# Two instruction orders and one split load in a two-layer adapter, attention and router kernel

## The chip, the cores and the metric

The kernel runs on one core of a Trainium2 chip. The metric is the device time of one execution in microseconds (us); for a kernel timed several times it is the median. A profiled execution of the same program gives the trace that all times of single instructions come from; its span, from the first to the last instruction, is a little shorter than its device time.

## The reference

The input x has 8 batches of 128 tokens with 512 features, float32. What is computed, cut to what matters:

```python
# layer 0
c = einsum('bsi,boi->bso', x, weight[adapter_ids])            # one 512 x 512 matrix per batch
x = x + c @ base_w.T + base_b + 2 * (top-2 gated sum of 8 rank-16 experts on c)
# layer 1, attention: 32 query heads, 8 key/value heads, head size 128
q, k, v = x @ Wq.T, x @ Wk.T, x @ Wv.T
q, k = rope(rmsnorm(q)), rope(rmsnorm(k))                      # positions start at cache_seqlens
kc, vc = k_cache[block_table], v_cache[block_table]            # 16 pages of 32 tokens per batch
o = softmax(mask(q @ concat(kc, k).T / sqrt(128))) @ concat(vc, v)
o = o @ Wo.T
# layer 1, router: 64 experts of rank 8, top 16
x = x + 2 * ((o @ A_w.T) * gate(o)) @ B_w.T
```

## The kernel before

**Stages.** The first stage (L0, lines 367 to 648) goes over the 8 batches: product with the batch's adapter matrix (`l0_adapter`, L494), copy (L503), products with the gate and low-rank matrix (L511) and the base matrix `bww` (L516), expert gating, and the new x, normed by a power of two and transposed into `xo` (L578). The second stage (L1, lines 751 to 1073) is the attention, the third (lines 1076 to 1145) the end of the router. The whole instruction order is written out by hand: each engine executes its instructions in the order in which the code emits them, and waits on semaphores where data or buffers need it.

**Loads of L0.** `l0_load(b)` issues on SyncE (SP) the transposed x of a batch (`xT`, L377; for batch 0 on ScalarE's queue) and its adapter matrix (L382), chosen by a register. Batch 0's matrix is loaded in two halves of its columns, all others whole. Behind batch 0's matrix SP issues `glw`, `bww`, then batch 1's `xT` and matrix.

**Units and turns.** Attention is cut into 32 steps (4 pairs of key/value heads by 8 batches) and each step into 2 units, 64 units in all; unit u belongs to step `u // 2`. Call `iteration(u)` turn u. Turn u does, for its unit's 4 query heads: `scores` (L788 against the cached keys `kt`, L791 against the new keys), `mask_exp` (L801 on VectorE reads the scores, adds the mask and takes the row minimum; L812 on ScalarE is the exponential), `normalize` (L817 on VectorE, L818 on GpSimd) and `blocks` (L823, a transpose of 32 x 32 blocks on VectorE into the tile `pb`). The scores of a head take a PSUM tile `s` of two; head 2 needs the tile of head 0, head 0 of the next unit that of head 2. When all four heads' blocks and a unit's rotated q and k (`blocks_qk`, L774) are in `pb`, `exchange_out` (L835) writes it to DRAM in four DMAs, two issued by SP and two by ScalarE; this tile in DRAM is `px`. In the next turn `exchange_in` (L845, L848) reads it back as `qkb` (q and k of the unit two after) and `pT`. There is one `pb`, so `blocks_qk` of a turn waits until the last turn's `px` has landed.

**What else a turn holds.** `values` (L868) of the unit two before, `evict_o` (L879, ScalarE, tile `oT`) and `output` (L890) of the unit three before, `project` (L259: q, k and v of units to come, three or four of seven products of a scheme that multiplies sums of halves) and `heads_qk` (L855, ScalarE: `qkb` to `qkT`, which the next turn's scores read). At the end of turn u stand `norms(u + 3)` and `rotate(u + 3)`:
- `norms`: five squares with a sum (L308) and a scaled copy `vn` (L310) on ScalarE, then on GpSimd mean and epsilon (L312, `ss`) and the power -0.5 (L314, `rs`);
- `rotate`: on VectorE L326 twice for q, L340 twice for k (these need `rs`), L343 and L344. It reads tables that `make_tables` (L233) makes on GpSimd. Its result is read by `blocks_qk(u + 3)` in turn u + 1.

The order at the end of a turn is: `normalize` of head 3, `norms`, `blocks` of heads 2 and 3, `exchange_out`, `rotate`. In turns 0 to 2 `project_whole` (L292) stands in place of `project`. `sums_q` (L163, VectorE) adds quarters of a projection matrix; `sums_x` (L168 to L171, GpSimd) does so for x.

**Keys and values.** The 16 key pages of the next step are gathered one DMA each by SP (`gather`, L193 and L194), 8 in each of a step's two turns: three at the turn's start, then `exchange_in`'s two DMAs, which wait for `px`, then five. Value rows come by GpSimd (`gather_v`, L204). `load_y` (L143) and the store of y (L914) are issued by SP in a step's first turn, after the pages and before `exchange_out`. Projection matrices of the next pair of heads are loaded by GpSimd (`load_q`, L153) in four turns of every sixteen.

The lines that decide the order of the pages:

```python
first = u % GH * NPP // GH                 # GH = 2, NPP = 16
if pages:
    gather(st + 1, first, first + 3)
if on(u - 1):
    exchange_in(u - 1)
if pages:
    gather(st + 1, first + 3, first + NPP // GH)
```

Of the kernel before, what the change touches and what calls it, by code (L numbers as in the profile page):

```python
# [16 lines left out]
P = 128  # L17
B = 8
S = 128
DM = 512  # L20
# [6 lines left out]
PAGES, PSIZE, NPP = 64, 32, 16  # L27
# [3 lines left out]
GH = 2  # L31
# [26 lines left out]
def adaln_ffn_kernel(  # L58
# [59 lines left out]
        out=nw, in_=norm_w.rearrange("o (t d) -> o t d", t=2).to_broadcast([P, 2, D])  # L118
# [39 lines left out]
    def sums_q(g, *tees):  # L158

        w = wq_t[g]  # L160
        for t in tees:
            to, x, y = {3: (5, 3, 1), 2: (4, 5, 0), 4: (6, 2, 4), 1: (1, 1, 0)}[t]
            nc.vector.tensor_tensor(w[:, to], w[:, x], w[:, y], ALU.add if t == 2 else ALU.subtract)  # L163
# [19 lines left out]
    def gather(step, first=0, end=NPP):  # L183
        hf, b = divmod(step, B)
        if first == 0:
            kv_t[step] = (
                kvp.tile([P, NPP, GH, PSIZE], F32, tag="kt", name=f"kt_{step}"),
                kvp.tile([P, LC, GH * D], F32, tag="vt", name=f"vt_{step}", bufs=3),
            )
        kt, vt = kv_t[step]  # L190
        for j in range(first, end):
            at = b * NPP + j
            page = nc.sync.value_load(pg[0:1, at : at + 1])  # L193
            nc.sync.dma_start(  # L194
                out=kt[:, j, :, :].rearrange("p g t -> p (g t)"),
                in_=kc[hf, ds(page, 1)].rearrange("o p f -> p (o f)"),
            )
# [26 lines left out]
    NU = len(units)  # L224
# [122 lines left out]
    def rotate(u):  # L347
        rotate_q(u)
        rotate_k(u)
# [17 lines left out]
    with ExitStack() as l0:  # L367
# [6 lines left out]
        def l0_load(b):  # L374
            xT = p2.tile([P, NC, S], F32, tag="xT", name=f"xT_{b}", bufs=3)
            eng = nc.scalar if b == 0 else nc.sync
            eng.dma_start(out=xT, in_=xt[b].rearrange("(c p) n -> p c n", p=P))  # L377
            wt = wt_home.pop(b)
            a = nc.sync.value_load(ids[0:1, b : b + 1])
            half = DM // 2 if b == 0 else DM  # L380
            for n in range(0, DM, half):
                nc.sync.dma_start(  # L382
                    out=wt[:, :, n : n + half],
                    in_=w0[ds(a, 1), :, n : n + half].rearrange("o (c p) n -> p (o c) n", p=P),
                )
            loaded[b] = [xT, wt]

# [49 lines left out]
        for i in range(QD):  # L437
            nc.gpsimd.dma_start(
                out=vpg[i * 32 : (i + 1) * 32], in_=vpages[i : i + 1].to_broadcast([32, B * LC])
# [311 lines left out]
    with ExitStack() as l1:  # L751
# [63 lines left out]
        def normalize(u, h):  # L815
            den = den_t.pop((u, h))
            nc.vector.reciprocal(den, den)  # L817
            nc.gpsimd.tensor_scalar(p_t[u, h], p_t[u, h], den, 1.0, ALU.mult, ALU.mult)  # L818
# [135 lines left out]
        def iteration(u):  # L954
# [16 lines left out]
                slots = (1, 2, 6) if four else (4, 5, 3)  # L971
            st = u // GH
            pages = on(u) and 1 < st + 1 < NQ * B
            first = u % GH * NPP // GH
            if pages:
                gather(st + 1, first, first + 3)
            if on(u - 1):
                exchange_in(u - 1)
            if pages:
                gather(st + 1, first + 3, first + NPP // GH)  # L980
            if pages:
                gather_v(st + 1, u % GH * LC // GH, (u % GH + 1) * LC // GH)
            if on(u + 3) and u % GH == 1:
# [12 lines left out]
            for h in range(REP):  # L996
                if on(u):
                    scores(u, h)
                    mask_exp(u, h)
                    if h > 0:  # L1000
                        normalize(u, h - 1)

                    if h == 1:
                        if u == 2:
                            sums_q(0, 1)
                        elif u == 3:
                            sums_q(1, 3, 2)
                        elif u == 4:
                            sums_q(1, 4, 1)
                        elif r in (10, 11, 12, 13) and u < NU - 8:  # L1010
                            sums_q(group + r // 12, *((3, 2), (4, 1))[r % 2])
                    if h == 2:
                        new_pb(u)
                        if u + 2 in range(3, NU):
                            blocks_qk(u + 2, u)
                    if h > 1:
                        blocks(u, h - 2)
                    if h == 1 and u == NU - 5:
                        f_fold(f[1])
                    if h == 2 and fb is not None:  # L1020
                        yT_t[fb] = f_turn(fb, *f)
                if on(u - 3):
                    output(u - 3, h)
                if h > 0 and slots:
                    project(k, j, slots[h - 1 : h])

                if u < 3 and h in (1, 3):
                    project_whole(1, *[(0, 1, h // 2), (1, h // 2, 1), (1, h // 2, 0)][u])
# [13 lines left out]
                load_o(group - 1, r * 2 - 2, r * 2)  # L1042
            if NU - 8 < u < NU - 2:
                f_weights(u - NU + 7)
            if on(u):
                normalize(u, REP - 1)
            if 3 < u + 3 < NU:
                norms(u + 3)
            if on(u):
                blocks(u, REP - 2)  # L1050
                blocks(u, REP - 1)
                exchange_out(u)
            if 3 < u + 3 < NU:
                rotate(u + 3)
                if four and slots:
                    project(k, j, (7,))
# [167 lines left out]
```

## Time and profile before

| | |
|---|---|
| Median of 3 runs | 1245.48 us (1244.46 to 1246.58) |
| Profiled execution | 1245.63 us |
| Its span | 1243.9 us |
| TensorE (PE) busy | 1225.1 us, 98% |
| VectorE (DVE) busy | 902.7 us, 73% |
| GpSimd (POOL) busy | 588.8 us, 47% |
| ScalarE (ACT) busy | 506.2 us, 41% |
| DMA moved | 298.99 MB, mean 240 GB/s |
| Granted TensorE clock, mean | 0.997 |

PE's weight loads (PEld) overlap its matmuls. A float32 matmul of the program shows as two records, so "x8" is four of them. In a timeline a line gives the start in us, the time in us, engine, source line and operation, output <- inputs, and in brackets how long the engine was idle before it and what released it. SPq and ACTq are DMA issues by SP and ScalarE. In a table of windows a line gives the stretch, its length, the busy time of PE, PEld, DVE, ACT and POOL, the granted PE clock, the DMA engines' busy share and GB/s. The releaser of a wait is inferred, and where several things were waited for it is the one that came last by the record.

### The profile page before, as it was taken

What the parts mean: (1) busy time and instruction counts of PE and PEld (TensorE: products, weight loads), DVE (VectorE), ACT (ScalarE), POOL (GpSimd) and SP (SyncE); (2) the same over time, 40 slices, a digit from 0 to 9 for tenths busy, and PEclk for the clock granted to TensorE, in tenths of its full rate; (3) what the DMA queues carried; (4) which work ended last, traced back from release to release, by engine and by line L of the source; (5) the groups of instructions that cost most, each with busy time, mean ns of one, the idle gap of its engine ahead of it and who ended that gap; (6) DMA issues with size and microseconds to landing.
All of it is one profiled execution on the core that took longest, in us unless ns stands there. A gap on an engine that the chain in (4) does not pass through costs nothing.

```text
span 1243.9 us, 15966 instructions
## 1 busy us (share of the span) xinstructions
PE 1225.1 (98%) x3851; PEld 650.3 (52%) x3851; DVE 902.7 (73%) x2045; ACT 506.2 (41%) x1457; POOL 588.8 (47%) x687
## 2 busy tenths in 40 slices
PE   9999899999999999999999999999999999999998
PEld 7765455544555555554555545555455555555444
DVE  2546798888877777788877777799777777787522
ACT  1334444444444444444444444444444444443211
POOL 2443465575544445554545544555545444553100
PEclk9999899999999999999999999999999999999999
DMA  9922777788777877888878877888878777887512
GB/s 302 303 79 94 224 235 247 246 272 284 254 239 255 262 250 240 282 287 259 279 246 263 254 251 246 290 280 278 259 244 287 244 235 230 258 280 256 185 51 85
DMA packets 211553, 298.99 MB, mean 240 GB/s; under 512 B 84547, under 2 KB 122180, under 8 KB 211460
## 3 DMA queue, kind: packets, MB, share of 16 engines
q1 hardware_dynamic: 179620, 205.69, 52.9%
q10 hardware_dynamic: 18960, 52.21, 11.9%
q0 software_dynamic: 12880, 40.08, 9.8%
q8 instruction: 31, 0.51, 0.2%
q14 instruction: 62, 0.51, 0.1%
HBM read 183.54 MB, written 114.36 MB: 239 GB/s over the span
## 4 chain that ended last, share of the span: by engine, by line
PE 89%; DMA 3%; DVE 3%; ACT 1%; issue 1%; POOL 1%; SPq 1%; ACTq 0%; DVEq 0%; POOLq 0%
PE o L868 20%; PE p L259 18%; PE s L788 17%; PE y L890 16%; PE s L791 4%; PE cp L494 2%; PE p L292 2%; PE bp L516 2%; PE op L1121 2%; DMA px<-pb 2%; PE fz L700 2%; DMA kt<-in_kc 1%; PE cp L511 1%; ACT sq L308 1%; DVE pb L823 1%
## 5 line engine op out<-in xcount | busy, mean ns | idle before, releaser
L818 POOL TENSOR_SCALAR p<-p,den 128x640 f32<-128x640 f32 x256 | 210.2, 821 | 427.1 <-DVE den L817 426.6
L812 ACT ACTIVATE p<-p,low 128x640 f32<-128x640 f32 x256 | 211.9, 828 | 442.8 <-DVE den L817 293.6
L801 DVE CUSTOM_DVE_ANT_0 p<-s,mask,rs 128x640 f32<-128x640 f32 x256 | 223.8, 879 | 114.5 <-PE s L791 111.4
L259 PE MATMUL p<-wqkv,xo 128*128 128x384 f32 x784 | 280.4, 486 | 0.0
L788 PE MATMUL s<-kt,qkT 128*128 128x512 f32 x504 | 257.9, 593 | 5.0 <-issue 2.5
L890 PE MATMUL y<-wo,oT 128*128 128x512 f32 x512 | 261.3, 595 | 1.2 <-ACT oT L879 1.2
L868 PE MATMUL o<-pT,vt 128*128 128x512 f32 x512 | 230.2, 592 | 0.0
L823 DVE STREAM_TRANSPOSE pb<-p 128x640 f32<-128x640 f32 x256 | 211.0, 824 | 17.0 <-POOL p L818 17.0
L259 PEld LDWEIGHTS p<-wqkv,xo 128*128 128x128 f32 x784 | 148.9, 190 | 139.8 <-issue 72.7
L791 PEld LDWEIGHTS s<-qkT 128*128 128x128 f32 x504 | 95.8, 190 | 120.6 <-issue 120.6
L868 PEld LDWEIGHTS o<-pT,vt 128*128 128x128 f32 x512 | 97.3, 190 | 110.3 <-issue 95.2
L204 POOL DMA_INDIRECT vt<-in_vc,vrow x128 | 136.1, 1063 | 39.7 <-issue 27.6
L788 PEld LDWEIGHTS s<-kt,qkT 128*128 128x128 f32 x504 | 94.8, 190 | 100.6 <-issue 57.5
L314 POOL TENSOR_TENSOR rs<-ss,mhalf 128x5 f32<-128x5 f32 x64 | 99.8, 1559 | 5.3
L308 ACT ACTIVATE sq<-c 128x128 f32<-128x128 f32 x320 | 98.8, 309 | 8.1
L791 PE MATMUL s<-qkT 128*128 128x128 f32 x504 | 96.8, 274 | 0.0
L879 ACT COPY oT<-o 128x512 f32<-128x512 f32 x64 | 37.5, 585 | 142.1 <-PE o L868 139.4
L890 PEld LDWEIGHTS y<-wo,oT 128*128 128x128 f32 x512 | 78.4, 192 | 6.5 <-issue 4.3
L262 DVE TENSOR_TENSOR c<-c,p 128x384 f32<-128x384 f32 x84 | 45.3, 539 | 30.4 <-PE p L259 30.4
L868 PE MATMUL o<-pT,vn 128*128 128x512 f32 x128 | 65.4, 592 | 0.0
L308 ACT ACTIVATION_READ_ACCUMULATOR sq<-c 128x1 f32 x320 | 59.7, 187 | 0.0
L340 DVE SCALAR_TENSOR_TENSOR ca<-c,rs,tab 128x128 f32<-128x128 f32 x64 | 24.4, 380 | 43.0 <-POOL rs L314 43.0
(180 smaller groups left out, 1205.7 us busy)
## 6 DMA issues: line engine op xcount, KB each, us to landing
pT<-px SPq DMA_DIRECT2D x64, 1280.0 KB, 6.6
px<-pb SPq DMA_DIRECT2D x122, 400.0 KB, 5.8
px<-pb ACTq DMA_DIRECT2D x122, 400.0 KB, 6.3
qkb<-px SPq DMA_DIRECT2D x61, 320.0 KB, 3.5
kt<-in_kc SPq DMA_DIRECT2D x512, 32.0 KB, 4.5
wqkv<-in_wqkv POOLq DMA_DIRECT2D x32, 384.0 KB, 5.6
yd<-ya SPq DMA_DIRECT2D x24, 256.0 KB, 2.0
wo<-in_wo POOLq DMA_DIRECT2D x12, 512.0 KB, 4.6
```

Source lines behind the costliest of these rows:

```text
L204: nc.gpsimd.indirect_dma_start(out=kv_t[step][1][:, c, :], out_offset=None, in_=vc, in_offset=bass.IndirectOffsetOnAxis(ap=vrow[:, hf, at ...
L259: nc.tensor.matmul(out=ps, lhsT=xo[:, pr, x, c, :], rhs=w[:, c, :], start=(c == 0), stop=(c == 1))
L308: nc.scalar.activation(sq, cs[:, at : at + D], AF.Square, accum_out=ss[:, h : h + 1])
L314: nc.gpsimd.tensor_tensor(rs, ss, mhalf, ALU.pow)
L788: nc.tensor.matmul(out=s[:, :L], lhsT=qkT[:, h, :], rhs=kt[:, :, g % GH, :], start=True, stop=True)
L791: nc.tensor.matmul(out=s[:, L:NK], lhsT=qkT[:, h, :], rhs=qkT[:, REP, :], start=True, stop=True)
L801: nc.vector.tensor_tensor_reduce(out=p, in0=s_t.pop((u, h))[:, :NK], in1=mask_t[st], scale=rs_t[u][:, h : h + 1], scalar=BIG, op0=ALU.add, ...
L812: nc.scalar.activation(p, p, AF.Exp, bias=low, scale=-1.0, accum_out=den)
L818: nc.gpsimd.tensor_scalar(p_t[u, h], p_t[u, h], den, 1.0, ALU.mult, ALU.mult)
L823: nc.vector.transpose(pb_t[u][:, :, h * w : (h + 1) * w].rearrange("p i (j a) -> p j i a", a=32), p_t.pop((u, h)).rearrange("p (j i a) -> ...
L868: nc.tensor.matmul(out=o, lhsT=vt[:, c, j * D : (j + 1) * D] if c < LC else vn_t.pop(u), rhs=pT[:, c], start=(c == 0), stop=(c == LC),)
L890: nc.tensor.matmul(out=y_t[st], lhsT=oT_t[u][:, h, :], rhs=wo_t[g][:, h, :], start=(h == 0 and j == 0), stop=(h == REP - 1 and j == GH - 1),)
```

## The change

Three things are changed; nothing is computed differently.

- Unit 4: `norms(4)` moves from the end of turn 1 to the end of turn 0, `rotate(4)` from the end of turn 1 into turn 2, behind `mask_exp` and `normalize` at head 1. The `sums_q(0, 1)` that stood there moves to the end of turn 2, before `normalize` of head 3.
- Key pages: 10 in a step's first turn (three, the exchange's two reads, seven) and 6 in its second (three and three), in place of 8 and 8.
- Batch 0's adapter matrix is loaded in four pieces of 128 columns in place of two of 256.

The matmuls of PE and their order stay the same.

```diff
-            half = DM // 2 if b == 0 else DM
-            for n in range(0, DM, half):
+            part = DM // 4 if b == 0 else DM
+            for n in range(0, DM, part):
                 nc.sync.dma_start(
-                    out=wt[:, :, n : n + half],
-                    in_=w0[ds(a, 1), :, n : n + half].rearrange("o (c p) n -> p (o c) n", p=P),
+                    out=wt[:, :, n : n + part],
+                    in_=w0[ds(a, 1), :, n : n + part].rearrange("o (c p) n -> p (o c) n", p=P),
                 )
...
-            first = u % GH * NPP // GH
+            first, end = ((0, 10), (10, NPP))[u % GH]
             if pages:
                 gather(st + 1, first, first + 3)
             if on(u - 1):
                 exchange_in(u - 1)
             if pages:
-                gather(st + 1, first + 3, first + NPP // GH)
+                gather(st + 1, first + 3, end)
...
                     if h == 1:
                         if u == 2:
-                            sums_q(0, 1)
+                            rotate(4)
...
+            if u == 2:
+                sums_q(0, 1)
             if on(u):
                 normalize(u, REP - 1)
-            if 3 < u + 3 < NU:
+            if u == 0:
+                norms(4)
+            elif 4 < u + 3 < NU:
                 norms(u + 3)
             if on(u):
                 blocks(u, REP - 2)
                 blocks(u, REP - 1)
                 exchange_out(u)
-            if 3 < u + 3 < NU:
+            if 4 < u + 3 < NU:
                 rotate(u + 3)
```

## The prediction

> **What bounds the kernel now.** I read the page first (busy shares, chain), then the waits of TensorE, then the timelines around each wait. One profiled execution ran 1245.63 us, its span is 1243.9; the three timed runs have the median 1245.48, 0.15 below it. I sum against 1245.63 and take 0.15 off at the end. Differences under 0.2% (2.5 us) can't be told from no change here.
>
> ```profile
> PE 1225.1 (98%) x3851; PEld 650.3 (52%) x3851; DVE 902.7 (73%) x2045; ACT 506.2 (41%) x1457; POOL 588.8 (47%) x687
> PE 89%; DMA 3%; DVE 3%; ACT 1%; issue 1%; POOL 1%; SPq 1%; ACTq 0%; DVEq 0%; POOLq 0%
> ```
>
> PE is busy 98%, and the change leaves its instructions and their order alone. So only PE's idle 18.8 us, and stretches at half clock, can be won. PE's waits (engine, line, releaser; total, times, longest) name what this change can touch:
>
> ```profile
> PE s L788 <- DVE low L801: 4.1, 1, 4.1
> PE s L788 <- issue: 2.5, 1, 2.5
> PE s L788 <- DMA px<-pb: 1.6, 1, 1.6
> PE cp L494 <- DMA wqkv<-in_w: 1.1, 1, 1.1
> PE s L788 <- DMA kt<-in_kc: 0.4, 1, 0.4
> ```
>
> The rest is start, tail and small L0 waits that no edit reaches.
>
> **Part A: unit 4's norms and rotation.** The 4.1 us are in turn 2. Scores of head 2 need the PSUM pair of head 0, freed by the masked read (L801) on DVE; that stands behind rotate(4) (L326 to L344), which waits for POOL's rs, which waits for ACT's five squares:
>
> ```profile
> 140.59 0.35 DVE L340 SCALAR_TENSOR_TENSOR ca<-c,rs,tab 128x128 f32<-128x128 f32 x1 [1.35 <-POOL rs L314]
> 142.04 0.88 DVE L801 CUSTOM_DVE_ANT_0 p<-s,mask,rs 128x640 f32<-128x640 f32 x1
> 142.99 2.07 PE L788 MATMUL s<-kt,wt 128*128 128x512 f32 x2 [4.09 <-DVE low L801]
> 146.00:147.00 1.00, 1.00 (x3) 0.34 (x2) 1.00 (x4) 0.49 (x1) 0.41 (x1) 0.50 0.32 17
> 148.00:149.00 1.00, 1.00 (x5) 0.60 (x4) 0.90 (x4) 0.00 (x0) 0.00 (x0) 1.00 1.07 369
> ```
>
> The last two are windows: third number from the end is PE's granted clock. After the stall PE ran at 0.50 until 147.8: 142.99 to 150.17 took 7.18 us, where the same two scores and one projection at full clock take 1.08 + 1.08 + 2.58 = 4.74. So the stall costs 4.09 + 2.44 = 6.5 us.
>
> After the change DVE leaves turn 1 at 138.0 and goes straight to L801 (0.80 from one to the next): 138.0 to 138.9, just as PE finishes its projection at 138.9. The stall is gone here. What the moved steps cost:
> - Turn 0: five squares (0.43 each) and vn (0.39) are 2.55 us of ACT, from 124.8 (end of a copy) to 127.3. Behind them on ACT are px(0)'s two DMA issues, now at 126.46. At 153.17 ACT issued such a DMA 0.25 before its vn began, so I expect 126.6: 0.15 late, at most 0.9 if it waits for vn. POOL's ss and rs (0.3 + 1.2) and the tables (1.45) then end at 129.9, so p(1,0) starts 1.2 after its present 128.63; its transpose runs only at 133.08, so that is covered.
> - Turn 2: rotate(4) is 2.7 us of DVE (137.98 to 139.23 and 140.59 to 142.04) between the reads of heads 1 and 2; it ends near 142.9, head 2's read 143.8. Then DVE needs pb free, which px(1) holds until it has landed.
> - sums_q(0,1) (1.3 mean) goes to turn 2's end; its reader comes in turn 4. Covered; it delays rotate(5) by about 1, but that waits for rs(5).
>
> What is late next is the exchange:
>
> ```profile
> 145.45 0.54 SPq L845 DMA_DIRECT2D qkb<-px  x1
> 150.75 0.73 ACT L855 COPY qkT<-qkb 128x640 f32<-128x640 f32 x1
> 154.66 0.59 ACT L879 COPY oT<-o 128x512 f32<-128x512 f32 x1 [0.86 <-PE o L868]
> 158.68 0.87 DVE L801 CUSTOM_DVE_ANT_0 p<-s,mask,rs 128x640 f32<-128x640 f32 x1
> ```
>
> px(1) leaves when turn 1's blocks are done (138.0) and lands at 145.4. Nothing in the change hastens that. Then qkb(3) (median 3.5 + 0.5 queue), ACT's copy to qkT(3) from 149.4 to 150.1. PE, freed of the stall, would be ready for turn 3's scores at 148.2: it waits 1.9. Then ACT does norms(5) (2.45 us), two issues (0.8), and only then oT(0): ready at 153.6, where PE could use it at 151.2: another 2.4. rs(5), rotate(5) and L801 of unit 3 follow qkT(3): 150.1 instead of 151.45, so that read ends at 158.2 where it now ends at 159.55. PE started its third score pair at 159.63, right behind it. So of 6.5 us only 1.3 is left. The two new waits lie 1 us apart in a stretch of 5.4 us, and the clock may fall again: PE stopped at 138.9 and by the windows 0.50 was granted from about 140.9, 2.0 us later. Then PE's 4.1 us of work from 153.6 to that score pair takes up to 2.4 more, as after 142.99, or half of that; it would end at 157.7, so 0.55 is cover. That leaves a gain of 0.7 or a loss of 0.5. Bounds for A: gain 1.3 to loss 2.2 (all 4.1 us at half clock, third pair at 161.8). I take a gain of 0.6, near the middle case.
>
> [...]
>
> **Part B: ten pages, then six.** The waits at 307.11 (1.57), 575.00 (2.46) and 874.70 (0.38) are first scores of a step, behind turns in which weights are loaded. PE there needs qkT, which ACT had ready 4 us before, and kt. The releaser names ("issue", px) are not what feeds it; the last pages are:
>
> ```profile
> 565.52 3.71 SPq L194 DMA_DIRECT2D kt<-in_kc  x5
> 575.00 1.10 PE L788 MATMUL s<-kt,qkT 128*128 128x512 f32 x2 [2.46 <-issue]
> ```
>
> Five issues in 3.71 us are 0.84 apart, so the last left at 568.9, 6.1 before PE started. With two pages fewer behind qkb and pT, the last leaves 1.69 sooner. If it lands 1.69 sooner: 307.11 wins all 1.57, 575.00 wins 1.69 of 2.46, 874.70 all 0.38: 3.6 us. Bounds: nothing (landing set by pT's 1.28 MB and the weights ahead of it, not by issue) to 4.4 (lighter queue, all gone). I take 3.6: in the chain the last page before 874.70, issued at 870.15, landed 4.30 later, the median landing of all pages (4.5), so issue time decided there.
> Cost: in even turns SP issues 7 pages after pT, 1.69 more, ahead of load_y, the y store and px. Where pages end at 281.8 and px leaves at 287.61 that is covered. The tightest are turn 2 (pages to 150.9, px 152.00: 0.6 late) and the turn with pages to 854.1, y store 855.01, px 855.88: 0.8 late. That px carries q and k two turns ahead: px of 152.00 was read back at 159.98 and copied by ACT only at 167.84. So nothing; without that cover, 1.4 in all.
>
> **Part C: the first adapter matrix in four.** PE starts cp(0) at 8.04 after 1.06 idle. A 256 KB piece needs fewer bytes before it lands, so the first product could start up to 1.06 earlier. But:
>
> ```profile
> 13.67 0.30 PEld L516 LDWEIGHTS bp<-bww,cT 128*128 128x128 f32 x2 [0.16 <-DMA bww<-in_base_w]
> 17.24 0.37 SPq L377 DMA_DIRECT2D xT<-in_xt  x1
> 17.38 1.95 PE cp L494 x16
> ```
>
> PE then waits for bww at 13.65, and the second matrix landed at 17.2 (SP's L377 had waited 1.4 us for it) with PE needing it at 17.38. Gains before 13.65 are lost there. And SP issues two more DMAs (0.52 each) ahead of bww and the second matrix, and the matrix has 2048 rows of 512 bytes for 1024 of 1 KB. Later landings pass through, as PE has no gap from 13.7 to 76. Bounds: a gain of 0.2 (bww a little sooner) to a loss of 1.0 (both issues in full). From 6 us on the DMA share is 1.0, so most of the issue delay is hidden in the queue: I take a loss of 0.4.
>
> [...]
>
> **Sum.** 1245.63 - 0.6 (A) - 3.6 (B) + 0.4 (C) = 1241.8; less 0.15: 1241.7.
>
> **Rivals.**
> 1. The stalls only move: the clock falls in turn 3 (A gains 0), the pages land hardly sooner (B 1.0), C loses 0.4. 1245.5 - 1.0 + 0.4 = 1244.9. For it: pT and weights are in the same engines ahead of the pages. Against: the last page before 874.70 took 4.3, not 6.
> 2. All of it is won: 6.5 + 4.4, C nothing: 1245.5 - 10.9 = 1234.6. It needs qkT(3) by 148.2, so px(1) and qkb together 2 us faster. Against: DMA share 1.0 at 142 to 144.
> 3. Slower: DMA rows of 512 bytes cost as much each as rows of 1 KB. From 3 to 6 us the engines were 0.62 busy at 116 GB/s; were those 1 KB rows, one took 0.62 x 16 / 116 = 86 ns. 1024 more are 1024 x 0.086 / 16 = 5.5 us, through bww and the second matrix to PE, plus 2.4 at half clock as above: 1241.7 - 0.4 + 7.9 = 1249.2. It decides once the extra exceeds what A and B win, 4.2. Against: from 2 to 3 us 231 GB/s went at share 0.82, mostly xT's 512-byte rows: 28 ns each.
>
> **Chances.** Forecast 0.58, own range 1239.8 (A 1.3, B 4.4, C nothing) to 1243.2 (A nothing, B 2.7, C 0.4); rival 1 0.22; rival 2 0.10; rival 3 0.10. Leaving out rivals 2 and 3, the range is 1239.5 (C gaining 0.2) to 1245.5 (rival 1 with C at its 1.0). Faster (below 1243.0): 0.56 + 0.10 = 0.66. Slower (above 1248.0): rival 3 less its milder end, 0.08. Same: 0.26.
>
> **What would show it.** Right: no wait of PE on L801 near 143, head 0's read at 138; new waits near 150 for qkT and near 153 for oT; L801 of unit 3 near 157.4; the 307 and 874 waits gone, 575 under 1 us; cp(0) at 7.1 but cp(1) at 17.4 to 18.4. Wrong: px(0) issued by ACT after 127 (A's chain late by that), first-score waits unchanged (B), or cp(1) after 19 (C).

## The result, and the profile after

The change makes the kernel slightly slower: 1247.45 us (median of 22 executions, 1241.54 to 1251.87) against 1245.2 for the kernel before on the same chip (22 executions); ratio 1.0015 with the 95% interval [1.0004, 1.0026]. The forecast was 1241.7, range 1239.5 to 1245.5. Its profiled execution ran 1248.47, span 1246.7: 2.8 above before's. Executions of one kernel spread over some 10 us, so a single profile is read turn by turn, not by its end.

The page of the changed kernel, the two lines that answer to those of before:

```profile
PE 1228.2 (99%) x3851; PEld 652.5 (52%) x3851; DVE 901.5 (72%) x2045; ACT 506.1 (41%) x1457; POOL 590.2 (47%) x687
PE 84%; DMA 5%; DVE 4%; ACT 2%; issue 2%; POOL 2%; SPq 1%; ACTq 0%; DVEq 0%; POOLq 0%
```

PE is busy 3.1 us longer with the same matmuls. Some 2.6 of it lies in L0 and in turns 2 and 3, where more of them ran at half clock (PE worked 8.6 us at 0.50, before 4.8); the rest is spread over the run. The end's chain runs through PE 5% less, and through DMA, DVE and ACT more. Its waits (engine, line, releaser; total, times, longest):

```profile
PE y L890 <- ACT oT L879: 5.3, 6, 1.9
PE s L788 <- ACT qkT L855: 3.0, 1, 3.0
PE bp L516 <- DMA bww<-in_base_w: 1.5, 1, 1.5
...
PE s L788 <- DVE low L801: 0.6, 1, 0.6
PE cp L494 <- DMA wqkv<-in_w: 0.6, 1, 0.6
```

The 4.1 on L801 and the first-score waits of 2.5, 1.6 and 0.4 are gone, as was meant. New are bww, qkT and more of oT. In before's profile one more wait, of 0.61 at 272.02, is put down to oT but belongs to a first score: L788 reads no oT, its qkT had been ready for 5.8 us, and a page landed 0.24 ahead of it. So before's waits for pages were 5.0 us, not the 4.4 that the prediction counted.

**Where the time went.** The same PE instruction of both traces is set side by side (changed minus before):

| point | difference |
|---|---|
| batch 1's first product (L494; 17.31 before) | +2.92 |
| last product of `xo` in L0 (L292, 102.72) | +2.85 |
| last product of unit 1's values (L868, 170.99), "end of turn 3" below | +4.56 |
| past 322 | +3.20 |
| past 590 | +1.26 |
| past 1072 | +0.75 |
| end (1174.11) | +2.99 |

So in this profile the adapter pieces (C) cost 2.85 and unit 4 (A) 1.71; the pages (B) win 3.8 from turn 3 to 1072; and 2.2 are lost by 1111.62, where PE waits 1.86 for a copy to oT that stands behind the gating of the router's first batch (L723 on ACT). No other profile of this study has that last wait, those with A and B included (e4, e18), so it is not laid to the change; whether other executions of the changed kernel have it is not known.

**L0.** SP's issue of bww and PE's work on it, before:

```profile
4.27 0.83 SPq L411 DMA_DIRECT2D bww<-in_base_w  x1
13.68 3.70 PE L516 MATMUL bp<-bww,cT 128*128 128x512 f32 x8
```

The same and more after, then PE's granted clock in windows:

```profile
5.94 0.76 SPq L411 DMA_DIRECT2D bww<-in_base_w  x1
6.96 1.99 PE L494 MATMUL cp<-xT,wqkv 128*128 128x128 f32 x16
9.50 2.19 PE L494 MATMUL cp<-xT,wqkv 128*128 128x128 f32 x16 [0.55 <-DMA wqkv<-in_w]
15.08 5.32 PE L516 MATMUL bp<-bww,cT 128*128 128x512 f32 x8 [1.52 <-DMA bww<-in_base_w]
20.23 1.95 PE L494 MATMUL cp<-xT,wqkv 128*128 128x128 f32 x16
```

```profile
14.00:15.00 1.00, 0.00 (x0) 0.00 (x0) 0.71 (x7) 0.30 (x1) 0.00 (x0) 0.98 1.07 361
16.00:17.00 1.00, 1.00 (x3) 0.38 (x2) 0.83 (x8) 0.00 (x0) 0.00 (x0) 0.50 1.06 390
18.00:19.00 1.00, 1.00 (x4) 0.38 (x3) 0.00 (x0) 0.00 (x0) 0.00 (x0) 0.82 1.06 355
```

The first product starts at 6.96, 1.08 sooner. But bww is issued at 5.94 (4.27 before) and PE starts on it at 15.08 (13.68 before); the clock then is 0.50 from 14.95 to 18.36, and bp takes 5.32 where it took 3.70. So the 2.85 are 1.62 of half clock and 1.2 of later landing.

**Turns 2 and 3.** Before, px(1) left here, and was read back at 145.45:

```profile
138.09 0.79 SPq L835 DMA_DIRECT2D px<-pb  x2
```

Timeline of several engines after, in order of time; subtract 2.85 to compare with before:

```profile
129.64 0.34 ACTq L835 DMA_DIRECT2D px<-pb  x1
130.02 0.83 ACTq L835 DMA_DIRECT2D px<-pb  x1
140.79 1.11 POOL L204 DMA_INDIRECT vt<-in_vc,vrow  x1 [0.17 <-issue]
141.43 0.84 DVE L801 CUSTOM_DVE_ANT_0 p<-s,mask,rs 128x640 f32<-128x640 f32 x1
141.53 0.79 SPq L835 DMA_DIRECT2D px<-pb  x2
142.33 1.13 PE L788 MATMUL s<-kt,wt 128*128 128x512 f32 x2
150.02 0.54 SPq L845 DMA_DIRECT2D qkb<-px  x1
154.74 1.96 PE L788 MATMUL s<-kt,qkT 128*128 128x512 f32 x2 [2.96 <-ACT qkT L855]
157.63 0.36 ACTq L835 DMA_DIRECT2D px<-pb  x1
158.03 0.58 ACT L879 COPY oT<-o 128x512 f32<-128x512 f32 x1 [1.01 <-DMA kt<-in_kc]
158.67 2.08 PE L890 MATMUL y<-wo,oT 128*128 128x512 f32 x2 [1.54 <-ACT oT L879]
```

Unit 2's first masked read is at 141.43 (138.58 on before's clock) and PE goes on without a stall. px(1) leaves at 141.53 and its readback is issued at 150.02: 8.49 us, before it was 7.36. PE waits 2.96 for qkT and 1.54 for oT(0), and the clock is at half for 6.8 us:

```profile
154.00:155.00 1.00, 0.26 (x1) 0.26 (x2) 1.00 (x3) 0.99 (x4) 0.38 (x1) 0.95 1.01 376
157.00:158.00 1.00, 0.13 (x1) 0.00 (x0) 0.47 (x1) 0.02 (x1) 0.92 (x2) 0.50 0.99 222
161.00:162.00 1.00, 1.00 (x3) 0.34 (x2) 1.00 (x2) 0.00 (x0) 0.92 (x2) 0.64 0.93 262
```

The fall is at 154.90, the rise at 161.72 (a window whose clock is 0.95 was at 1.00 for nine tenths of it). PE worked 5.3 of these 6.8 us, so half of that, 2.6, is lost (bp above lost 1.62 in 3.28 us of half clock). Sum of A: 6.5 won; 2.96 + 1.54 + 2.6 and 0.65 at unit 2's second head lost: 1.25 of loss, beside 1.71 measured.

**First scores of steps**, the three places of before:

```profile
310.32 1.10 PE L788 MATMUL s<-kt,qkT 128*128 128x512 f32 x2 [0.22 <-PE o L868]
576.33 1.02 PE L788 MATMUL s<-kt,qkT 128*128 128x512 f32 x2
875.01 1.10 PE L788 MATMUL s<-kt,qkT 128*128 128x512 f32 x2
```

No wait of a score above 0.22 is left between turn 3 and the end. In exchange the waits for oT between 180 and 1110 rise from 0.59 to 1.34.

### The profile page after: what moved, and what is told of

The parts are those of the page before. It is cut to its first block, busy times and chain, and to the rows that moved or that the text cites. A ratio compares the mean times of both kernels' runs of the same rounds, so it can differ in the third digit from the quotient of the medians.

```text
span 1246.7 us, 16005 instructions
## 1 busy us (share of the span) xinstructions
PE 1228.2 (99%) x3851; PEld 652.5 (52%) x3851; DVE 901.5 (72%) x2045; ACT 506.1 (41%) x1457; POOL 590.2 (47%) x687
## 4 chain that ended last, share of the span: by engine, by line
PE 84%; DMA 5%; DVE 4%; ACT 2%; issue 2%; POOL 2%; SPq 1%; ACTq 0%; DVEq 0%; POOLq 0%
PE o L868 19%; PE p L259 18%; PE y L890 16%; PE s L788 15%; PE s L791 4%; PE bp L516 2%; DMA px<-pb 2%; PE op L1125 2%; PE cp L494 2%; PE p L292 2%; PE fz L700 2%; ACT sq L308 1%; DMA kt<-in_kc 1%; DVE pb L823 1%; DMA bww<-in_base_w 1%
## 5 line engine op out<-in xcount | busy, mean ns | idle before, releaser
L801 DVE CUSTOM_DVE_ANT_0 p<-s,mask,rs 128x640 f32<-128x640 f32 x256 | 223.7, 879 | 108.8 <-PE s L791 106.0
L890 PE MATMUL y<-wo,oT 128*128 128x512 f32 x512 | 262.7, 598 | 5.3 <-ACT oT L879 5.3
L788 PE MATMUL s<-kt,qkT 128*128 128x512 f32 x504 | 259.4, 597 | 3.2 <-ACT qkT L855 3.0
L868 PE MATMUL o<-pT,vt 128*128 128x512 f32 x512 | 230.2, 593 | 0.0
L868 PEld LDWEIGHTS o<-pT,vt 128*128 128x128 f32 x512 | 97.5, 190 | 110.1 <-issue 95.0
L788 PEld LDWEIGHTS s<-kt,qkT 128*128 128x128 f32 x504 | 95.5, 191 | 98.7 <-issue 54.9
L890 PEld LDWEIGHTS y<-wo,oT 128*128 128x128 f32 x512 | 78.6, 192 | 11.3 <-ACT oT L879 6.8
L262 DVE TENSOR_TENSOR c<-c,p 128x384 f32<-128x384 f32 x84 | 45.3, 540 | 29.0 <-PE p L259 29.0
L868 PE MATMUL o<-pT,vn 128*128 128x512 f32 x128 | 65.4, 592 | 0.0
L774 DVE STREAM_TRANSPOSE pb<-ca 128x640 f32<-128x640 f32 x61 | 50.5, 827 | 10.8 <-DMA px<-pb 9.5
```

The costliest lines, as they stand in the source:

```text
L788: nc.tensor.matmul(out=s[:, :L], lhsT=qkT[:, h, :], rhs=kt[:, :, g % GH, :], start=True, stop=True)
L801: nc.vector.tensor_tensor_reduce(out=p, in0=s_t.pop((u, h))[:, :NK], in1=mask_t[st], scale=rs_t[u][:, h : h + 1], scalar=BIG, op0=ALU.add, ...
L868: nc.tensor.matmul(out=o, lhsT=vt[:, c, j * D : (j + 1) * D] if c < LC else vn_t.pop(u), rhs=pT[:, c], start=(c == 0), stop=(c == LC),)
L890: nc.tensor.matmul(out=y_t[st], lhsT=oT_t[u][:, h, :], rhs=wo_t[g][:, h, :], start=(h == 0 and j == 0), stop=(h == REP - 1 and j == GH - 1),)
```

## Experiments

Eighteen kernels were run, each beside the kernel before on the same chip. "End of turn 3" and "end" are differences to before's profile at the points of the table above, from one profiled execution each. The end of L0 is +0.5 in some of the two-piece kernels and 0 in others, which is no effect of an edit: e3 and e12 are the same kernel. Where a loss of A is given "with L0 taken off", it is the difference at the end of turn 3 less that at the end of L0. Ratios are of timed runs in 5 rounds, for e5 to e8 in 3, with 95% intervals; "in rounds" below means these. Among eighteen intervals about one that leaves out 1 is to be expected by chance.

| kernel | L0 | end of turn 3 | end | ratio of timed runs |
|---|---|---|---|---|
| the change | 2.85 | 4.56 | 2.99 | 1.0015 [1.0004, 1.0026] |
| e1 C only | 1.72 | 1.06 | 8.16 | 1.0014 [0.9990, 1.0038] |
| e2 A only | 0.52 | 3.65 | 3.26 | 1.0015 [0.9994, 1.0036] |
| e3 B only | 0.45 | -0.11 | -3.77 | 0.9984 [0.9966, 1.0002] |
| e4 A and B | 0.49 | 2.83 | -0.04 | 1.0037 [1.0015, 1.0059] |
| e5 rotation only | 0.50 | 1.50 | -0.28 | 1.0016 [0.9996, 1.0037] |
| e6 norms behind px | 0.59 | 3.33 | 2.96 | 1.0013 [0.9993, 1.0032] |
| e7 C on two queues | 1.15 | 2.41 | 0.68 | 0.9992 [0.9974, 1.0010] |
| e8 B, two rotations moved | 0.44 | 1.37 | 2.80 | 1.0007 [0.9984, 1.0030] |
| e9 e5 with PE kept busy | -0.11 | -0.84 | 0.28 | 0.9981 [0.9968, 0.9994] |
| e10 e8, early oT | -0.20 | -0.83 | -2.10 | 0.9994 [0.9975, 1.0013] |
| e11 e10 with PE kept busy | -0.22 | 0.90 | 0.34 | 1.0012 [0.9992, 1.0033] |
| e12 B only again | -0.12 | -0.70 | -2.39 | 1.0019 [0.9993, 1.0044] |
| e13 A, late gathers | 0.04 | 1.14 | 2.81 | 1.0013 [0.9992, 1.0033] |
| e14 A mended | -0.22 | -0.24 | -0.71 | 0.9983 [0.9966, 1.0001] |
| e15 A mended, B | -0.21 | -0.34 | 1.57 | 1.0008 [0.9988, 1.0028] |
| e16 before, PE kept busy | 0.22 | -0.73 | -3.13 | 0.9985 [0.9967, 1.0004] |
| e17 e16 and B | 0.06 | -0.51 | -1.46 | 0.9998 [0.9978, 1.0018] |
| e18 the change mended | -0.03 | -0.50 | 1.27 | 1.0002 [0.9984, 1.0019] |

### The parts alone (e1 to e4)

Each kernel is the kernel before with one part of the diff shown above (e4 with A and B).

> Only the four column pieces of batch 0's matrix. Theory 1 (from the trace after the change): base matrix bww lands about 1.4 us later, TensorE idles there for about 1.5 us, its clock is halved, and the whole program is 2.5 to 3 us slower (about 1248), shown by the first L292 of batch 7 and all later work shifted by 2.8. Rival (the recorded sum): the issue delay is mostly hidden, 0.4 us slower.

Measured: 1248.42 us; the interval of the ratio takes in 1. L0's end is 1.72 later, with the clock at 1.00 all through, though PE waited 1.82 for bww:

```profile
14.85 3.70 PE L516 MATMUL bp<-bww,cT 128*128 128x512 f32 x8 [1.82 <-DMA bww<-in_base_w]
```

So in the profiles the four pieces cost 1.2 to 1.7 by themselves, and up to 2.85 where the clock falls. The rest of this profile's 8.16 are other things: a page wait of 4.83 near 277 with half clock behind it (the scores at 277.30 took 2.05), and one of 1.89 near 315 (scores of 1.10).

> Only norms(4) in turn 0, rotate(4) in turn 2 and sums_q(0,1) at turn 2's end. Theory 1: the wait of 4.1 us on L801 turns into waits on qkT and oT in turn 3, with half clock in turn 3 in place of turn 2: 1 to 2 us slower than before (about 1246.5). Rival (the recorded sum): 0.6 us faster. Second rival: the loss in the whole change came only with the seven pages (a DMA issue of ScalarE that waits for a page), so that this part alone gains 0.5 to 1.3 us.

Measured: 1248.61. A loses 3.1 by the end of turn 3, without the changed matrix and without the seven pages: waits of 0.76 (L801), 3.13 (qkT) and 1.21 (oT), and 10.2 us at half clock. Theory 1 had the sign; the size is over it. The gain that the second rival allowed is not there either.

> Only ten and six key pages. Theory 1: the waits of the first score pair of a step (307, 575 and 875 us) go, 3.5 to 4.5 us faster (about 1241). Rival: what is won there is lost near the end, where in the whole change TensorE waited 1.9 us for oT at 1111 us: 1.5 to 2.5 us faster.

Measured: 1244.09. In the profile -3.77, as theory 1 has it: waits of scores fall from 5.0 to 0.2 us, while those for oT rise from 0.6 to 2.2. In rounds it is 1.65 faster, the rival's figure, with an interval that takes in 1; the profiled execution was the fastest of the twelve.

> Units and pages changed, batch 0's matrix in two pieces as before. Theory 1 (the three parts add up): the whole change less C, 2.85 us below it, 0.5 us faster than before or equal (1244.5 to 1245.5). Rival (recorded sum): 4 us faster than before.

Measured: 1249.13, 3.4 slower than before and not the 1244.5 to 1245.5 of theory 1. The profile fits the theory (A loses 2.3 by the end of turn 3, B wins 2.9 after it), but its execution, too, was the fastest of the twelve. With the old matrix load this kernel is no faster in rounds than the whole change, so C's cost is seen in profiles only.

### What makes A lose (e5, e6, e13)

```diff
 e5: norms(4) stays at the end of turn 1; rotate(4), sums_q(0, 1) as in the change
 e6: part A, but
-            if u == 0:
-                norms(4)
...
                 exchange_out(u)
+            if u == 0:
+                norms(4)
 e13: part A, but
-            if pages:
+            if pages and u != 2:
                 gather_v(st + 1, ...)
...
+                    if h == 2 and u == 2:
+                        gather_v(st + 1, 0, LC // GH)
```

> Only the rotation of unit 4 is moved into turn 2 (and sums_q(0, 1) to that turn's end); unit 4's norms stay at the end of turn 1, pages and adapter matrix are as before. Theory 1 (part A loses by the norms in turn 0: they stand on ScalarE ahead of px(0)'s issues, about 0.7 us, and they free GpSimd, so that the value gathers leave about 2 us earlier and run beside px(1), which then takes 8.6 us to land where it took 7.4): here px(1) leaves within 0.2 us of before's 138.1 and lands within 0.3 of 145.5; no wait on L801 near 143; TensorE waits some 1.9 us for qkT near 150 and up to 2.4 for oT; the end of turn 3 lies between 1.3 us earlier and 0.5 later than before's (the run with all of part A was 3.1 later). The whole: 1244.5 to 1246. Rival (the chain qkT, norms(5), oT with its half clock is enough for the loss, wherever the norms of unit 4 stand): still 2 us or more later at the end of turn 3.

Measured: px(1) left at 138.71, 0.12 late once L0's 0.50 is taken off, and was read back at 146.12, 7.41 later. PE's waits are the two that the prediction named (1.9 and 2.4):

```profile
150.82 1.13 PE L788 MATMUL s<-kt,qkT 128*128 128x512 f32 x2 [1.86 <-ACT qkT L855]
154.22 2.08 PE L890 MATMUL y<-wo,oT 128*128 128x512 f32 x2 [2.06 <-ACT oT L879]
```

A still loses 1.0 (1.50 less L0's 0.50): neither the gain that theory 1 allowed nor the rival's 2. The clock was 0.50 from 153.28 to 160.10, and PE worked 5.9 of that.

> Part A alone, with one change: unit 4's norms in turn 0 are issued behind px(0) and not ahead of it. Theory 1 splits in two here: px(0) leaves ScalarE at its old time, so px(1) leaves about 0.7 us earlier than with all of part A, at 138.1 plus what the first layer adds; but the gathers are still early, so px(1) still takes about 8.6 us. End of turn 3: 1 to 2 us later than before (3.1 with part A as it is). Rival 1 (the gathers do no harm, px(0)'s delay is all): px(1) lands 7.4 after its issue, and the end of turn 3 is as with the rotation alone. Rival 2 (neither matters): 3 us later, as with part A as it is.

Measured: px(1) left at 139.05 and took 8.86; PE waited 3.34 for qkT; A loses 2.7. So px(0)'s delay on ACT is worth some 0.4 of e2's loss of 3.1, and the later landing of px(1) some 1.7, since e5, where it lands on time, still loses 1.0.

> Part A alone, with one change: in turn 2 GpSimd issues the two value gathers behind the second head's work and not at the turn's start. In every kernel with the norms in turn 0 these gathers left at 138.3 to 138.6 (140.8 in the changed kernel, whose times are 2.3 later), with px(1), and px(1) took 8.5 to 9.1 us to land; in every kernel with the norms at turn 1's end they left at 140.7 or later and px(1) took 7.4. Theory: the gathers are the reason, and px(1) takes 7.3 to 7.6 us here; TensorE's wait for qkT near 151 is then about 2.2 us (3.1 with part A alone); the end of turn 3 is 1 to 1.5 us earlier than with part A alone. Rival: px(1) still takes 8.5 us or more, so something else that the norms' place changes slows it.

px(1)'s issue and its readback, SP's timeline, part A alone and then with the late gathers:

```profile
139.32 0.79 SPq L835 DMA_DIRECT2D px<-pb  x2
...
147.97 0.54 SPq L845 DMA_DIRECT2D qkb<-px  x1
```

```profile
138.81 0.79 SPq L835 DMA_DIRECT2D px<-pb  x2
145.85 0.54 SPq L845 DMA_DIRECT2D qkb<-px  x1
```

8.65 becomes 7.04 by moving the gathers alone: they are the cause. All twenty profiles agree: where the first gather left 0.7 us ahead of px(1), 8.49 (the change), 8.65 (e2), 9.06 (e4), 8.86 (e6); where it left 2 to 3 us after it, 7.29 to 7.52 (before and thirteen others); where it left 7 us after it, 7.04 (e13, e18). Before, GpSimd came to the gathers later because unit 4's `rs` stood ahead of them. The first gather in before, then in e2:

```profile
140.74 1.18 POOL L204 DMA_INDIRECT vt<-in_vc,vrow  x1 [0.19 <-issue]
138.58 1.10 POOL L204 DMA_INDIRECT vt<-in_vc,vrow  x1 [0.17 <-issue]
```

The wait for qkT fell to 1.52; that for oT rose to 3.38, because px(2)'s second issue on ACT was held until 154.31, here with five pages ahead of it and not seven. The end of turn 3 is 2.5 us earlier than with A alone (2.0 with L0 taken off).

### The clock (e9, e16)

```diff
 e9: as e5, and at turn 3, ahead of scores(3, 0) 14 and ahead of output(0, 0) 15 of these;
 e16: the kernel before, and ahead of scores(2, 2) 32 of these
+    nc.tensor.transpose(busy[:, :S], ident, ident)     # busy: a free PSUM bank
```

> The rotation of unit 4 alone moved, as in the run with the rotation alone, and TensorE given work in its two waits of turn 3: 14 transposes of the identity into a free PSUM bank ahead of the first scores (for qkT, 1.86 us) and 15 ahead of the first output product (for oT, 2.06 us). Theory: the half clock in turn 3 (granted 0.50 for 6.8 us in the run with the rotation alone, of which TensorE worked 5.8, so 2.9 lost) follows from these waits; with the transposes the clock stays at 1.00 through turn 3 and its end is 2.4 to 2.9 us earlier than in that run, that is 0.9 to 1.4 earlier than before's. The whole: 1244 to 1245. Rival (the clock falls there whether TensorE idles or not, or the 29 transposes push the work out as much as they save): granted 0.50 again or the end of turn 3 at 1.5 later than before's.

Measured: 1244.45, ratio 0.9981 [0.9968, 0.9994], the only kernel that is faster than before with its whole interval. PE's waits and a window:

```profile
150.16 1.12 PE L788 MATMUL s<-kt,qkT 128*128 128x512 f32 x2 [0.36 <-ACT qkT L855]
153.31 1.13 PE L890 MATMUL y<-wo,oT 128*128 128x512 f32 x2 [0.16 <-ACT oT L879]
```

```profile
153.00:154.00 1.00, 0.84 (x4) 0.46 (x3) 0.00 (x0) 0.26 (x1) 0.92 (x2) 1.00 0.95 250
```

The clock stays at 1.00 through turn 3, which ends 2.34 earlier than in e5 (1.73 with L0 taken off), less than the 2.4 to 2.9 expected: 1.10 now go to a wait for L801 at 158.76.

> The kernel before, with 32 transposes of the identity (0.121 us each at full clock, 3.87 in all) into a free PSUM bank ahead of unit 2's scores of head 2, where TensorE stood still for 4.09 us in turn 2; nothing is taken from the work and nothing moved. Theory: the half clock that followed the stall (2.44 us in before's profile) goes, the stall itself stays: the end of turn 3 is 2 to 2.5 us earlier than before's, the whole 1243 to 1243.5, 0.998. Rival: the clock falls all the same, or the transposes end later than the masked read and push the scores out: end of turn 3 within 0.5 us of before's.

Measured: 1243.53, 0.9985 [0.9967, 1.0004].

```profile
139.08 3.66 PE L1000 MATMUL busy<-ident 128*128 128x128 f32 x32
143.33 1.12 PE L788 MATMUL s<-kt,wt 128*128 128x512 f32 x2 [0.60 <-DVE low L801]
...
154.71 1.12 PE L890 MATMUL y<-wo,oT 128*128 128x512 f32 x2 [0.97 <-ACT oT L879]
```

The clock stayed at 1.00 through the whole profile, and PE was 1.96 ahead by the last product of unit 0's values (2.2 with L0 taken off). Then 0.97 went to a wait for oT(0) that before's slower PE did not meet, and 0.73 is left: between the theory and the rival.

### Adapter pieces on two queues (e7)

```diff
+            a2 = nc.scalar.value_load(ids[0:1, 0:1]) if b == 0 else None
...
-                nc.sync.dma_start(
+                second = b == 0 and n >= DM // 2
+                (nc.scalar if second else nc.sync).dma_start(
```

> The first adapter matrix in four pieces, the third and fourth issued on ScalarE's queue; nothing else is changed. Theory (the two more issues on SP's queue, ahead of bww and the second matrix, make these later by the 1.7 us that they take): bww is issued near 4.3 us and lands near 13.7, TensorE's wait for it is back to about 0.2 us, and the first layer's end lies within 0.5 us of before's (1.7 us later with four pieces all on SP at full clock). Rival (rows of 512 bytes cost the DMA engines more for each byte, whoever issues them): bww is issued near 4.3 but still lands near 14.5 or later, and the first layer ends 1 us or more later.

Measured: SP issued bww at 4.29 and PE did not wait for it; the second batch's product starts at 17.84, 0.53 later than before, and L0 ends 1.15 later (0.6 by the two-piece kernels with +0.5). In e18, with the same pieces on the same queues, batch 1 starts at 17.27 and L0 ends at -0.03. So most or all of the loss is SP's issue order, not the 512-byte rows.

### Mending the later waits (e8, e10, e11, e14, e15)

```diff
 e8: part B; rotate(4) in turn 2; norms(5) behind evict_o(0) in turn 3, rotate(5) in turn 3 at head 1
 e10: e8, and values(0), evict_o(0) right behind heads_qk(3) in turn 2
 e11: e10 and 14 transposes ahead of scores(3, 0)
 e14: e11 without part B, norms(5) at its old place; e15: e14 and part B
```

> Part B as in the change; unit 4's norms at the end of turn 1 as before and its rotation in turn 2; unit 5's norms behind the copy to oT(0) at turn 3's start and its rotation in turn 3 (sums_q(1, 3, 2) to that turn's end); the matrix in two pieces. Theory 1: part B takes 3.6 to 4.2 us off, at first scores of steps; px(1) lands as before, nothing stands on ScalarE ahead of oT(0), so that of the waits in turn 3 only that for qkT, 1.9, is left; the end of turn 3 is 2 to 3 us earlier than before; the whole 1239 to 1240.5. Rival (the clock falls after that wait too, and takes what is left): end of turn 3 within 1 us of before, the whole 1241 to 1242.5, no better than part B alone.

Measured: 1247.65. Waits of 1.90 (qkT) and 2.40 (oT, because px(2)'s second issue on ACT stood ahead of it, by the record for a page), half clock from 152.74 to 159.56; turn 3 ends 1.37 late, and B won nothing after it (see below). Both theories miss.

> As the run with part B, the rotation of units 4 and 5 moved and norms(5) in turn 3, but the copy to oT(0) now stands on ScalarE right behind qkT(3), ahead of px(2)'s issues, one of which waited 1.5 us for a page there. Theory: the wait for oT(0) near 154.5 (2.40 us) is gone, the wait for qkT (1.9) stays; the end of turn 3 is 1 us (clock falls to 0.50 all the same) to 4 us (it does not) earlier than before's, where it was 1.4 later; the whole 1239.5 to 1243, with part B's 3.8 at the first scores of steps. Rival: TensorE then waits for the masked read (L801) of unit 3's second head instead, and the end of turn 3 is not earlier than before's.

Measured: 1243.97, ratio 0.9994. The wait for oT(0) is gone, the half clock lasts 3.4 us only, and turn 3 ends 0.83 earlier, just short of the theory's 1 to 4; a wait of 1.55 for a sum on DVE (L262), late behind rotate(5), is new.

> The kernel of the run just above with 14 transposes of the identity ahead of turn 3's first scores, so that TensorE does not idle while it waits for qkT. Theory: clock 1.00 all through turns 2 and 3; of the 6.5 us of before's stall in turn 2 only the 1.9 for qkT are left; the end of turn 3 is 3.5 to 4.6 us earlier than before's; with part B the whole is 1237.5 to 1239.5. Rival: the same as without the transposes to within 0.5 us, so idleness was not what set the clock.

Measured: 1247.64. The clock stays at 1.00 until 165.48, PE is ahead, and loses it all to that sum, and then to half clock (0.50 from 166 to 168):

```profile
165.37 2.85 PE L259 MATMUL p<-wqkv,xo 128*128 128x384 f32 x4 [3.26 <-DVE c L262]
```

Turn 3 ends 0.90 late: the theory failed, on DVE's order and not on the clock.

> Part A's rotation with every later wait mended: unit 4's norms at turn 1's end, its rotation in turn 2; unit 5's rotation in turn 3 (sums_q(1, 3, 2) to that turn's end); the copy to oT(0) right behind qkT(3) on ScalarE, norms(5) behind it and ahead of px(2); 14 transposes of the identity ahead of turn 3's first scores. Pages and matrix as before. Theory: the clock stays at 1.00 in turns 2 and 3, and no wait above 0.6 us is left there; the end of turn 3 is 3.5 to 4.6 us earlier than before's; the whole 1241 to 1242.5. Rival: rotate(5), which now stands between the masked reads of turn 3's second and third heads, keeps VectorE from the sums (L262) that TensorE's products wait for, as in the two kernels with norms(5) in turn 3 (1.6 and 3.3 us there), and the end of turn 3 is no more than 2 us earlier.

Measured: 1244.90, 0.9983. The rival holds: rs(5) comes sooner, yet PE waits 2.25 for L262 at 164.23; turn 3 ends 0.24 earlier.

> The kernel of the run just above with part B. Theory: 3.5 to 4.6 us earlier at the end of turn 3 and 3 to 4 more at the first scores of steps: the whole 1238 to 1240, faster than before in the rounds (0.9945 to 0.997). Rival: part B's gain is taken back by waits for oT and half clock in single turns, as in its second profile, where 1.4 of 3.9 us were lost again: 1241 to 1243.

Measured: 1246.55, 1.0008: the rival's kind of loss, and more of it than its 1241 to 1243. ACT and PE, timeline:

```profile
288.64 2.44 ACTq L835 DMA_DIRECT2D px<-pb  x2
291.13 0.58 ACT L879 COPY oT<-o 128x512 f32<-128x512 f32 x1 [2.76 <-DVE sa L340]
```

```profile
291.76 2.07 PE L890 MATMUL y<-wo,oT 128*128 128x512 f32 x2 [3.28 <-ACT oT L879]
```

ACT's two issues of px took 2.44 where they usually take 0.84, the copy to oT stands behind them, PE waits 3.28 and then runs at half clock (0.50 still at 295 to 296): 6.3 us lost against before's trace over this turn. This loss isn't part B's alone: in e14, the same kernel without it, the two issues of this turn were held as well, and PE waited 1.38:

```profile
287.78 1.98 ACTq L835 DMA_DIRECT2D px<-pb  x2
```

### Part B again (e12, e17)

> Part B alone, once more, on the same chip as the three others, to tell whether its gain is the 3.8 us of its first profile (waits at the first scores of steps) or the 1.6 of its first timed rounds. Theory: 2 to 4 us faster than before in the rounds, 0.997 to 0.9985, and no wait above 1 us at a step's first scores. Rival: within 1 us of before, because the copies to oT wait behind px's second issue on ScalarE, which waits for one of the seven pages ahead of it: then waits for oT of 0.5 us or more appear in more turns than in before's profile.

Measured: 1246.11, ratio 1.0019 [0.9993, 1.0044], where the first rounds had 0.9984; the profile is 1.7 better past turn 3, with first-score waits of 1.34 and 0.63 and oT waits of 0.73 and 0.59. The rival holds.

> The kernel of the run just above with part B. Theory: 2 to 2.5 us from the clock in turn 2 and 2 to 3.8 from the first scores of steps: the whole 1239.5 to 1241.5, 0.9955 to 0.997. Rival: part B gives nothing in the rounds, as in its second timing (1246.1 beside 1246.0), since waits for oT come for those for pages: the whole as without it, 1243 to 1243.5.

Measured: 1244.54, 0.9998; e16 without part B had 0.9985. The rival (1243 to 1243.5) is nearer.

### The change with its three causes taken out (e18)

The change, with e7's queues, e13's late gathers, and 12 and 20 transposes in turn 3's two waits.

> The whole change, with the three causes of its loss taken out: the third and fourth piece of the adapter matrix on ScalarE's queue, turn 2's value gathers behind the second head's work, and 12 and 20 transposes of the identity in turn 3's two waits. Theory: the first layer's end at most 0.8 us later than before's (2.85 in the change), px(1) landing 7.0 to 7.6 us after its issue (8.5), clock 1.00 in turn 3, the end of turn 3 between 1 us later and 1.5 us earlier than before's (4.6 later in the change); the whole 1242 to 1245 (1247.45 the change). Rival: the change's loss lies elsewhere, in the rest of the run: 1246.5 or more.

Measured: 1246.59, 1.0002 [0.9984, 1.0019]. SP's timeline, then PE's:

```profile
4.41 0.86 SPq L413 DMA_DIRECT2D bww<-in_base_w  x1
```

```profile
13.79 3.60 PE L518 MATMUL bp<-bww,cT 128*128 128x512 f32 x8
17.27 2.02 PE L496 MATMUL cp<-xT,wqkv 128*128 128x128 f32 x16
```

Up to the end of turn 3 the theory holds: -0.03 after L0, px(1) in 7.04, clock 1.00, -0.50 at the end of turn 3 where the change had +4.56. In the rest of the run 1.8 are lost again: waits for oT (1.95, 0.69, 1.29 and 0.81) and the half clock behind the first (scores of 1.92 at 291.51, 1.02 at 459.14) outweigh the page waits that are gone. So the whole is at the rival's figure, and the rounds cannot tell it from before, nor, as the intervals overlap, from the change.

## Why the prediction was wrong, step by step

**A, forecast -0.6, measured +1.7 to +3.1 in profiles.** Right: the stall of 6.5 us goes; the next limits are qkT and then oT(0), and with px(1) on time they cost 1.86 and 2.06 (e5) beside 1.9 and 2.4 forecast; px(0)'s second issue on ACT ended 0.7 late, within the 0.9 named. Two steps failed. "px(1) leaves when turn 1's blocks are done and lands at 145.4. Nothing in the change hastens that": true, but something slows it. Moving `norms(4)` takes `ss` and `rs` off GpSimd's queue ahead of the value gathers, which then leave 2.7 us sooner (e2: 138.58, less L0's 0.52, beside 140.74) and run beside px(1), which lands 1.1 to 1.7 us later for it (e13 shows it by moving the gathers alone). The prediction followed ACT's and DVE's queues past the moved step and on GpSimd only `rs` itself. And the clock was taken at "the middle case", 1.2 us of loss; in every profile where both of A's waits were left to idle it fell, for 6.8 or 10.2 us but in e13 (3.4), with 2.6 us of loss in the change and 2.9 in e5 (e9 takes it out). With what e5 shows, its sum is -6.5 + 1.86 + 2.06 + 2.9 = +0.3 beside 1.0 measured; 0.7 stay unexplained.

**C, forecast +0.4, measured +1.2 to +2.9 in profiles.** Right: the first product starts at 7.0 (1.08 sooner in the change, 0.61 in e1, where the prediction allowed up to 1.06) and this is lost at bww. Batch 1's first product came at 20.23, past the 19 that the prediction named as a sign of being wrong. The failed step is "most of the issue delay is hidden in the queue": bww was issued 1.67 later and its product started 1.4 later, so hardly any was hidden. Cause: SP's order, since with two pieces on another queue bww is not waited for (e7, e18). The clock's fall, 1.62 in the change, was named under the third rival and left out of the sum. That rival's rows of 512 bytes as dear as 1 KB rows are refuted by e18: the same rows, and no loss.

**B, forecast -3.6, in profiles -3.8 to +1.9, in rounds about nothing.** In the change's own profile the figure comes out (3.8 by 1072), but that is luck. The step that failed is "I take 3.6": the term was read from the waits of one execution and taken as won in full. These waits come at other places and in other sizes in every execution, and behind them stands the next one, the copy to oT. Waits of PE of 0.2 us or more between 180 and 1110, means over the ten profiles without B and the ten with it: scores (L788) 3.9 and 0.9 us, output (L890, which waits for oT) 1.2 and 2.7. So B takes 2.9 and gives back 1.5. From the end of turn 3 to the end the ten profiles without B lose 0.3 against before's on the mean (-2.4 to +7.1), the ten with it win 0.7 (-3.7 to +1.9): the scatter is larger than the gain. In timed runs B gave 0.9984 and 1.0019 alone, and e4 beside e2, e15 beside e14 and e17 beside e16 are 1.0022, 1.0025 and 1.0013: no gain of 3 us, and a loss of up to 3 isn't excluded.

The prediction asked of B's cost ("So nothing") who waits for px, not who stands behind px's issues on ACT. That this place costs PE time is shown (e15: 3.28), but not that B makes it worse: pairs of px's issues on ACT that took more than 1.2 us between 180 and 1110 (0.84 is usual) number 31 in the ten profiles without B and 34 in the ten with it. A PE that is held up less at the pages comes sooner to the copy, and this alone may raise the waits for oT; e16, where PE was sped up without B, met one of 0.97 in turn 3. Which of the two it is stays open: a kernel with seven pages and px's issues off ACT was not tried.

**Sum.** In the profile +1.7 (A) + 2.85 (C) - 3.8 (B) + 2.2 (the wait at 1111, not the change's) = +3.0. In rounds, +1.9. In the profiles the sign went wrong because A and C each lost over 2 us more than their terms; in rounds neither A nor C alone is clear of 1, and the gain forecast for B, a ratio of 0.997, lies inside e3's interval but outside e12's.

## What to carry to other kernels

When a step is moved, write down for every queue that it leaves what now starts earlier, and ask what that runs beside: here two gathers set free put px(1) off by more than 1 us. For each DMA issue ask who stands behind it on the same engine if it is held, and whether a load put ahead of another one delays it by its issue time (bww was issued 1.67 later behind two more pieces). A wait read from one profile is one draw: look at several executions before its size becomes a term, and ask what limits next when it is gone. Here a stall on TensorE could have a second price, the half clock after it (2.44 us behind before's stall of 4.09, 2.6 in turn 3 of the change); transposes in waits that could not be removed kept the clock at 1.00 there (29 in e9, 32 in e16).

## What the hardware showed

The granted clock stayed at half for 3.4 us (the change in L0, 14.95 to 18.36; e10, 151.08 to 154.50), 6.8 (before, 140.93 to 147.76; the change, 154.90 to 161.72; e5, 153.28 to 160.10) or 10.2 (e2, 151.96 to 162.2). In the traces of before and of the change, the times from each fall or rise to the next (6.83 and 1095.68 us; 3.41, 136.53, 6.83 and 1085.44) are 2 and 321, and 1, 40, 2 and 318 times 3.4133 us, to 0.01; why was not shown. In the 3.41 us ahead of these falls PE idled 2.04 (before, 140.93), 2.07 and 2.95 (the change, 14.95 and 154.90). Two windows of before, the first up to the fall at 140.93, the second with the first 1.88 of PE's wait of 2.46 ahead of 575.00, which had no fall behind it (1.00 from 574.42 to 577.84):

```profile
137.52:140.93 3.41, 1.37 (x5) 0.49 (x3) 2.06 (x5) 1.06 (x5) 2.23 (x3) 1.00 0.69 208
571.01:574.42 3.41, 1.53 (x4) 0.38 (x2) 2.87 (x7) 0.58 (x1) 2.91 (x3) 1.00 1.01 350
```

In e5 each wait was shorter (1.86 and 2.06), the 3.41 us ahead of 153.28 held 2.07 of the two, and the clock fell there. In L0 the change lost its clock; e1, which waited 1.82 for bww, did not. So neither the length of one wait nor the idling within 3.41 us told here by itself whether half clock came; what decided it was not shown.

Two gathers of 0.13 MB each on GpSimd's queue made a 1.6 MB write 1.1 to 1.7 us later when they left beside it, though 0.26 MB take 0.67 us at the 390 GB/s of the busiest window shown above. No run here shows why the delay is larger than the bytes.
